# One layer with lagged attention beside a gated feed-forward: q and k of all tokens first, then v, z, o and Wout by halves, with v and z in three f32r passes

## The chip, the cores and the metric

The kernel runs on one core of a Trainium2 chip. The metric is the device time of one execution in microseconds, as the median of the runs. Durations below come from one execution that the hardware profiler recorded.

The engines are called by these names: PE (TensorE) multiplies matrices, DVE (VectorE) and ACT (ScalarE) work on elements, POOL (GpSimd) and SP (SyncE) issue most of the DMA transfers here. Each engine takes its instructions in the order in which they stand in the program.

## What is computed

`x` has 2048 tokens of 512 numbers, everything in f32. The layer is

```python
xn = layernorm(x)
q, k, v = (conv4(silu(xn @ W)) for W in (Wq, Wk, Wv))   # 2048 channels, causal conv over 4 tokens
z, a, b = xn @ Wz, xn @ Wa, xn @ Wb                     # a, b: one number per head
q, k = normalised(rope(q)), normalised(rope(k))         # 16 heads of 128
for s in range(4):                                      # four lags
    attn = sum_over_head(q * lag(k, s)) / sqrt(128)
    o += attn * sigmoid(lag(a, s) * b) * lag(v, s)
s = (o * rms(o) * norm_w * silu(z)) @ Wout
g = silu(relu(xn @ sign(up).T * up_scale) @ sign(down).T * down_scale * output_scale)
out = x + s * g
```

## The kernel before

Tokens go in four blocks of 512, heads in eight pairs (256 channels, two tiles of 128 by 512). Activations lie with channels on the partitions and tokens along the row. `xnT` holds the normalised tokens of all blocks in SBUF.

**Matmuls.** A matmul here has 128 rows of contraction, 128 output rows and 512 columns. The products with Wq, Wk, Wv, Wz and Wout are f32: 256 matmuls each. The profile shows every f32 matmul as two records. The feed-forward is f32r: its weights are signs, and `in_two_terms` splits the other operand into a high and a low term, so that 512 matmuls make up the up-projection and 512 the down-projection, each one record.

**Order.** `InOrder` keeps matmuls, all VectorE work, some ScalarE work (`act`) and some transfers (`pool`, `sp`) in the order in which the program names them. The rest is placed by the scheduler. `step(p, b)` runs pair `p`: q and k of block `b+1` (`queries`, `products`) beside v, z, o and Wout of block `b` (`values`, `weighted`, `gated_output`, `output_projection`). So a first row of eight steps with `b = -1` has q and k of block 0 alone. Beside those stands the feed-forward of block 0, in groups of four of its 16 hidden tiles: `ups` in even steps, `downs` in odd ones, half of it between pq and pk, and half after pk. There the signs are made on ScalarE from the raw weights (`sign`) and also written to `signs_dram`.

**Products and their sums.** `products` turns q for the four lags, multiplies q by the lagged k on VectorE and leaves the sum over the head to a matmul with 0/1 columns (`sum_dots`). In block 0 VectorE adds the two halves of the channels. In later blocks DMAs with accumulation, issued on POOL, do part of it: in an even step `pr1` onto `pr` (L452), then two half sums within `pr` (L469), which wait for the first to land; in an odd step two copies into the pair's tile (L472), then two half sums onto them (L473), which wait for the copies. `sq` (L435) is summed by such a DMA too.

**Between the stages.** The dots, the norms and the gates of a block become coefficients, which go to `co_dram` and come back spread over the partitions as `bc`; `weighted` multiplies v by them.

**Last stage.** After the last step come v, z, o and Wout of block 3, and then the feed-forward of blocks 1 to 3 with the signs loaded from `signs_dram` (`up`, `first_down`, `down`), its ends (`ends`) between.

Of the kernel before, what the change touches and what calls it, by code (L numbers as in the profile page):

```python
# [17 lines left out]
P = 128  # L45
# [3 lines left out]
D = 128  # L49
# [12 lines left out]
ROPE_BASE = 1000000.0  # L62
EPS_LN = 1e-5
# [18 lines left out]
def recurrent_layer(ctx: ExitStack, tc: tile.TileContext, a: dict, out: bass.AP):  # L82
# [10 lines left out]
    xnT = const.tile([P, KC, HALO + S], F32, name="xnT")  # L93
    ss_acc = const.tile([P, NT], F32, name="ss_acc")
# [23 lines left out]
    f_dram = dram.tile([TB, HID], F32, name="f_dram")  # L118
# [3 lines left out]
    att = ctx.enter_context(ExitStack())  # L122
    mm = ctx.enter_context(tc.tile_pool(name="mm", bufs=6, space=PSUM))
# [8 lines left out]
    nc.vector.memset(xnT[:, :, 0:HALO], 0.0)  # L132
# [15 lines left out]
    gates = {}  # L148

    def first_layer_norm():  # L150
# [23 lines left out]
        def transpose(c):  # L174
            tp = mm.tile([P, KC, P], F32, tag="mm", name=f"tp{c}")
            for k in range(KC):
                pe.transpose(tp[:, k, :], x_in[:, c, k * P : (k + 1) * P], ident)
            act.copy(xnT[:, :, HALO + c * P : HALO + (c + 1) * P], tp)
# [20 lines left out]
    def statistics(b, c):  # L199

        if c == 0:
            means[b] = qks.tile([P, TC, 2], F32, tag="mv", name=f"mv{b}", bufs=2)
            nc.sync.dma_start(xnT[:, :, HALO + b * TB : HALO + (b + 1) * TB], a["xT"][b])
# [26 lines left out]
    def centre(b):  # L230
# [9 lines left out]
        for k in range(KC):  # L240
            nc.gpsimd.dma_start(
                xnT[:, k : k + 1, HALO + b * TB : HALO + (b + 1) * TB], less, accum_op=ALU.add
            )

    def divide(b):

        rstd = qks.tile([P, TB], F32, tag="rq", name=f"rstd{b}", bufs=1)
        nc.sync.dma_start(rstd, ln_dram[b][1].partition_broadcast(P))
        at = xnT[:, :, HALO + b * TB : HALO + (b + 1) * TB]
        dve.tensor_tensor(at, at, rstd.unsqueeze(1).to_broadcast([P, KC, TB]), ALU.mult)  # L250

    def gate_products(b):
# [3 lines left out]
        for k in range(KC):  # L256
# [3 lines left out]
                xnT[:, k, HALO + b * TB : HALO + (b + 1) * TB],  # L260
# [70 lines left out]
    def first_product(to, second_half):  # L331

        pps = [mm.tile([P, TB], F32, tag="mm", name=f"pq{j}_0_0") for j in range(2)]
        for lo in range(0, TB, TB // 2):
            for j in range(2):
                for k in range(KC):
# [3 lines left out]
                        xnT[:, k, HALO + lo : HALO + lo + TB // 2],  # L340
# [8 lines left out]
    def project(n, p, b, to):  # L349
# [3 lines left out]
        for j in range(2):  # L353
            pp = mm.tile([P, TB], F32, tag="mm", name=f"p{n}{j}_{p}_{b}")
            for k in range(KC):
# [3 lines left out]
                    xnT[:, k, HALO + b * TB : HALO + (b + 1) * TB],  # L359
# [181 lines left out]
    gated = {}  # L541
    o_due = []

    def squares_of_o():
        while o_due:
            o_due.pop(0)()

    def values(p, b, raw):

        v = sum_with_halo(vs, "v", p, b)  # L550
        convolve(2, p, raw, v[:, :, HALO:])
        return v

    wos = {}

    def load_wo(p, b):
        wo = vs.tile([P, 2, HID], F32, tag="wo", name=f"wo_{p}_{b}", bufs=3)
        loads["by"].dma_start(wo, a["wo"][p])
        wos[p] = wo

    def gates_of_output(p, b):

        z = vs.tile([P, 2, TB], F32, tag="z", name=f"z_{p}_{b}", bufs=1)
        project("z", p, b, z)
        for j in range(2):
            nc.scalar.mul(z[:, j, :], z[:, j, :], norm_w[:, p, j : j + 1])
        return z

    def weighted(p, b, v):

        n = f"_{p}_{b}"
        parts = []
        for lo in range(0, LAGS, 2):

            bc = vs.tile([P, 2, TB], F32, tag="bc", name=f"bc{lo}" + n, bufs=3)
            for h in range(2):
                row = co_dram[b][lo : lo + 2, 2 * p + h, :]
                sp.dma_start(
                    bc[h * D // 2 : (h + 1) * D // 2], row.partition_broadcast(D // 2)
                )  # L580

            v0 = v[:, :, lo : lo + TB]
            v_lags = bass.AP(v0.tensor, v0.offset, [v0.ap[0], [1, 2], *v0.ap[1:]])
            te = vs.tile([P, 2, 2, TB], F32, tag=f"te{lo}", name=f"te{lo}" + n, bufs=1)
            dve.tensor_tensor(te, v_lags, bc.unsqueeze(2).to_broadcast([P, 2, 2, TB]), ALU.mult)
            parts.append(te)
        dve.tensor_tensor(parts[0], parts[0], parts[1], ALU.add)
        o = parts[0][:, 0]
        dve.tensor_tensor(o, o, parts[0][:, 1], ALU.add)


        o2 = xnT[:, p % 2 * 2 : p % 2 * 2 + 2, HALO : HALO + TB] if b else parts[1][:, 0]

        def square():
            (act if b else nc.scalar).activation(o2, o, AF.Square)
            if p == 0:
                pool.dma_start(o2_dram[b], o2)
            else:
                pool.dma_start(o2_dram[b], o2, accum_op=ALU.add)

        if b:
            o_due.append(square)
        else:
            square()
        return o

    def gated_output(p, b, o, z):

        oz = vs.tile([P, 2, TB], F32, tag="oz", name=f"oz_{p}_{b}", bufs=3)
        dve.tensor_tensor(oz, o, z, ALU.mult)  # L610
        gated[p] = oz
        if p % 2 == 1:
            pairs = gated.pop(p - 1), gated.pop(p)
            outputs_due.append(lambda *midway: output_projection(p, b, pairs, *midway))

    def output_projection(p, b, pairs, midway, chunks):

        ws = wos.pop(p - 1), wos.pop(p)
        for c in range(TC):
            if midway and c == chunks:  # L620
                midway()
            po = mm.tile([P, HID], F32, tag="mm", name=f"po{c}_{p}_{b}")
            for i, (of, w) in enumerate(zip(pairs, ws)):
                for j in range(2):
                    pe.matmul(
                        po,
                        of[:, j, c * P : (c + 1) * P],
                        w[:, j, :],
                        start=(i == 0 and j == 0),
                        stop=(i == 1 and j == 1),  # L630
                    )
            part = vs.tile([P, HID], F32, tag="part", name=f"part{c}_{p}_{b}", bufs=4)
            nc.scalar.copy(part, po)  # L633
            t = b * TC + c
            rows = s_dram[t * P : (t + 1) * P, :]
            if p == 1:
                nc.gpsimd.dma_start(rows, part)
            else:
                nc.gpsimd.dma_start(rows, part, accum_op=ALU.add)


    ss = xnT[:, :, HALO + TB : HALO + 2 * TB]

    def load_squares(b, j):

        if j:
            pool.dma_start(ss[:, b], o2_dram[b][:, j], accum_op=ALU.add)
        else:
            loads["by"].dma_start(ss[:, b], o2_dram[b][:, j])

    def output_projections(midway=None, chunks=TC // 2):
        if midway and not outputs_due:
            midway()
        while outputs_due:
            outputs_due.pop(0)(midway, chunks)
            midway = None


    first_due = []

    z_due = []

    def step(p, b, beside_q=None, beside_k=None):
# [4 lines left out]
        squares_of_o()  # L668
        if x_due:
            x_due.pop()()  # L670
        rv = with_halo(vs, "rv", "raw", 1, p, b) if p == b == 0 else None
        if beside_q:
            beside_q()
        if change and b:
            sum_squares(p)
            norms(b)
        due = bool(dots_due) and dots_due[0][-1]
        if change and not b:

            def beside_k():  # L680
                norms(b)
                norms_in_rows(b)

        products(p, b + 1, q, (lambda: norms_in_rows(b)) if change and b else None, beside_k)
        if z_due:
            z_due.pop()()
        if at:
            load(vs, "v", p, b)
            raw = raw_of(vs, "v", p, b, 1, rv)
        if first_due:  # L690
            first_due.pop()()
        if at:
            v = values(p, b, raw)

        def strips():

            if p and p % 2 == 0:
                sum_squares(p)
            if p == NP - 2 and b + 2 < NTB:
                gate_products(b + 2)  # L700
            if p == 1 and not at:
                gate_products(0)
            if due:
                sum_dots()

        z = []
        z_of = lambda: z.append(gates_of_output(p, b))

        early = p == 2 and b == 0
        if early:  # L710
            load(vs, "z", p, b)
            z_of()

        output_projections(strips if p % 2 == 0 or due else None)
        if change:
            coefficients(b)
        if at:
            if not early:
                load(vs, "z", p, b)
            load_wo(p, b)  # L720
            out_of = lambda: gated_output(p, b, weighted(p, b, v), z[0])
            if change:
                z_due.append(z_of)
                first_due.append(out_of)
            else:
                if not early:
                    z_of()
                out_of()
# [41 lines left out]
    def tokens(b):  # L770
        return xnT[:, :, HALO + b * TB : HALO + (b + 1) * TB]

# [403 lines left out]
```

## Time and profile before

| | |
|---|---|
| median of 3 runs | 1399.08 us (1397.86 to 1400.22) |
| span of the profiled execution | 1396.2 us |
| median less that span | 2.9 us |
| PE busy | 1384.6 us (99%) |
| DVE busy | 1179.6 us (84%) |
| ACT busy | 670.2 us (48%) |
| POOL busy | 235.8 us (17%) |
| DMA | 263.40 MB, mean 189 GB/s |

Times on the page and in the views are microseconds from the start of the span unless marked ns. A busy time is a union: records of pipelined matmuls overlap, so their mean duration is longer than the distance between their starts. "Idle before" is the time in which an engine stood before an instruction, with what ended it. "POOL a <- DMA b" in the table of waits reads: POOL, before its instruction on a, waited for the transfer b, with total, number and longest. Where a helper records an operation, its line is that of the helper (L76 before, L53 after).

### The profile page before, as it was taken

The numbers are of one execution on the slowest core, as the hardware profiler recorded it, in microseconds if no ns is written. First come the engines' busy times: TensorE is split into PE (matmuls) and PEld (weight loads), VectorE is DVE, ScalarE is ACT, GpSimd is POOL, SyncE is SP. The second block draws the span as 40 slices with busy tenths as digits, with TensorE's granted clock in tenths as the row PEclk, the third lists the DMA queues.
The fourth block names the chain that finished last, engine by engine and source line by source line (L and its number), as shares of the span: only waits on it lengthen the run. The fifth ranks groups of instructions, "written<-read, shape, count | busy, mean of one in ns | idle before, by whom it ended". The sixth has DMA issues, their size and how long they took to land.

```text
span 1396.2 us, 12500 instructions
## 1 busy us (share of the span) xinstructions
PE 1384.6 (99%) x3962; PEld 689.3 (49%) x3962; DVE 1179.6 (84%) x1183; ACT 670.2 (48%) x1309; POOL 235.8 (17%) x317
## 2 busy tenths in 40 slices
PE   9999999999999999999999999999999999999998
PEld 6555544444444444444444444444444444578886
DVE  7998989999899989998998999989994987337454
ACT  7566646546454564565545544545443443223122
POOL 2222111112213121113131112111111122200000
PEclk9999999999999999999999999999999999999999
DMA  9979577888988789889987798887848989754120
GB/s 319 329 177 206 127 186 178 231 199 205 237 194 190 164 165 243 219 201 197 214 183 163 171 235 203 210 183 179 179 91 204 272 219 243 145 192 139 33 91 31
DMA packets 104985, 263.40 MB, mean 189 GB/s; under 512 B 17812, under 2 KB 18324, under 8 KB 100568
## 3 DMA queue, kind: packets, MB, share of 16 engines
q0 software_dynamic: 36672, 108.02, 39.9%
q1 hardware_dynamic: 68248, 154.58, 37.1%
q8 instruction: 32, 0.52, 0.2%
q14 instruction: 33, 0.27, 0.1%
HBM read 159.77 MB, written 52.45 MB: 152 GB/s over the span
## 4 chain that ended last, share of the span: by engine, by line
PE 88%; DVE 5%; DMA 4%; ACT 1%; issue 1%; SPq 1%; POOL 0%; DVEq 0%; ACTq 0%; POOLq 0%
PE pq L76 15%; PE pk L76 15%; PE po L76 14%; PE pz L76 14%; PE pv L76 13%; PE pf L76 7%; PE ph L76 7%; DVE te L76 1%; PE dots L76 1%; DVE q L76 1%; PE squares L76 1%; DMA y<-s_dram 1%; DVE v L76 1%; DMA bc<-co_dram 1%; DVE k L76 0%
## 5 line engine op out<-in xcount | busy, mean ns | idle before, releaser
L76 PE MATMUL pq<-xnT,wq 128*128 128x512 f32 (+1 forms) x528 | 226.1, 580 | 0.8 <-ACT rstd L76 0.8
L76 PE MATMUL po<-wo,oz 128*128 128x512 f32 x512 | 225.6, 595 | 0.0
L76 PE MATMUL pz<-xnT,wz 128*128 128x512 f32 x512 | 225.2, 592 | 0.4 <-ACT rv L363 0.4
L76 PE MATMUL pk<-xnT,wk 128*128 128x512 f32 x512 | 225.2, 592 | 0.0
L76 PE MATMUL pv<-xnT,wv 128*128 128x512 f32 x512 | 225.2, 592 | 0.0
L76 DVE TENSOR_TENSOR te<-v,bc 128x2048 f32<-128x2048 f32 x64 | 143.9, 2288 | 33.8 <-ACT v L76 15.8
L76 DVE SCALAR_TENSOR_TENSOR k<-rk,conv_w,k 128x512 f32<-128x512 f32 x192 | 141.7, 751 | 30.5 <-ACT k L375 26.0
L76 PEld LDWEIGHTS pq<-xnT,wq 128*128 128x128 f32 x528 | 99.0, 189 | 123.6 <-issue 115.1
L76 PEld LDWEIGHTS po<-wo,oz 128*128 128x128 f32 x512 | 96.2, 190 | 126.5 <-issue 115.4
L76 PEld LDWEIGHTS pz<-xnT,wz 128*128 128x128 f32 x512 | 96.6, 189 | 123.9 <-issue 118.0
L76 PEld LDWEIGHTS pv<-xnT,wv 128*128 128x128 f32 x512 | 96.6, 189 | 123.8 <-issue 119.9
L76 PEld LDWEIGHTS pk<-xnT,wk 128*128 128x128 f32 x512 | 96.6, 189 | 120.6 <-issue 118.0
L76 DVE SCALAR_TENSOR_TENSOR q<-rq,conv_w,q 128x512 f32<-128x512 f32 x192 | 141.5, 749 | 17.1 <-ACT q L375 12.5
L76 DVE SCALAR_TENSOR_TENSOR v<-rv,conv_w,v 128x512 f32<-128x512 f32 x192 | 141.3, 750 | 6.4 <-ACT v L375 1.9
L76 DVE SCALAR_TENSOR_TENSOR q<-q,turns 128x1024 f32<-128x1024 f32 (+1 forms) x128 | 127.3, 1016 | 4.9 <-ACT q L76 2.6
L76 DVE TENSOR_TENSOR pr<-q,k 128x2048 f32<-128x2048 f32 x52 | 117.3, 2287 | 0.9
L76 DVE CAST hid_hi<-hid 128x512 fp32r<-128x512 f32 x52 | 22.4, 431 | 88.2 <-ACT hid L785 88.2
L785 ACT ACTIVATE hid<-ph,up_scale 128x512 f32<-128x512 f32 x64 | 43.5, 684 | 105.6 <-PE ph L76 104.3
L363 ACT ACTIVATE rq<-pq 128x512 f32<-128x512 f32 x62 | 36.8, 596 | 93.3 <-PE pq L76 93.2
L633 ACT COPY part<-po 128x512 f32<-128x512 f32 x64 | 36.9, 579 | 82.7 <-PE po L76 82.7
L76 PE MATMUL ph<-xs_hi,up 128*128 128x512 f32 x192 | 75.5, 393 | 0.0
L76 PE MATMUL ph<-xs_lo,up 128*128 128x512 f32 x192 | 74.7, 389 | 0.0
(154 smaller groups left out, 1744.6 us busy)
## 6 DMA issues: line engine op xcount, KB each, us to landing
bc<-co_dram SPq DMA_DIRECT2D x128, 256.0 KB
pr<-pr POOLq DMA_DIRECT2D x72, 256.0 KB, 6.9
wq<-in_wq_dram SPq DMA_DIRECT2D x32, 512.0 KB
wk<-in_wk_dram SPq DMA_DIRECT2D x32, 512.0 KB
sq<-sq POOLq DMA_DIRECT2D x32, 512.0 KB, 6.5
wv<-in_wv_dram SPq DMA_DIRECT2D x32, 512.0 KB
wz<-in_wz_dram SPq DMA_DIRECT2D x32, 512.0 KB
wo<-in_wo_dram SPq DMA_DIRECT2D x32, 512.0 KB
```

What stands on the lines that cost most here:

```text
L76: return self.tc.keep_in_program_order(getattr(self.engine, op)(*args, **kwargs))
L363: nc.scalar.activation(to[:, j, :], pp, AF.Silu)
L633: nc.scalar.copy(part, po)
L785: nc.scalar.activation(hid, ph, AF.Relu, scale=scale)
```

## The change

The work is laid out in two stages.

**Stage one: all q and k.** `step` has only q and k left. It runs for all four blocks, 32 steps in all, and each block has its own feed-forward beside it, as block 0 had before. `f_dram` grows to all tokens. In block 0 signs are made as before. For the later blocks each group of signs (1 MB) is read back from `signs_dram` by a `pool` transfer, called at the end of the step before the one that uses it, into one of two buffers:

```python
def fetch(b, g, which):
    if b:
        of = signs[which] = signs_of(b, g, which)     # tag "sign", bufs=2
        pool.dma_start(of, signs_dram[which][:, G * g : G * g + G])
        return
    ...
for b in range(NTB):
    for p in range(NP):
        ...
            step(p, b - 1, lambda: ups(...), lambda: ups(...))      # odd p: downs
        ...
        if n + 1 < len(groups) and groups[n + 1][0]:
            fetch(*groups[n + 1])
```

`xnT` is gone: each block of tokens has a tile of its own. Each block is also cut into three f32r forms, `h` (the value times 1 - 2^-13, rounded), `m` (value minus h) and `d` (h - 4096 m). `h` and `m` serve the feed-forward as its two terms, and all three are written to `forms_dram` (3 MB a block).

**Stage two: v, z, o, Wout**, for halves of 1024 tokens, eight pairs each (16 rounds). It starts when the pools of stage one are released. The forms of two blocks are loaded as `xf`; the weights of v and z are split on the way (`split_raw`: two ScalarE and two VectorE operations of 128 by 1024). A tile of v or z is then

```python
for k in range(KC):                       # form d with form d, 4 matmuls
    pe.matmul(pp, wd[:, k, ...], xf[b, 2][:, k], start=(k == 0), stop=(k == KC - 1))
nc.scalar.mul(pp, pp, -1.0 / (UNIT + 1.0))
for k in range(KC):                       # h with h and m with m, 8 matmuls on top
    for t, w in ((0, wh), (1, wm)):
        pe.matmul(pp, w[:, k, ...], xf[b, t][:, k], start=False, ...)
```

and 1 + 1/4096 goes into the scale of the Silu that reads it. That is 12 f32r matmuls for 4 f32 ones. `gated_outputs(i - 1)`, one half of an `output_projection`, and `raw_values(i)` follow each other in round `i`; Wout begins in round 3.

**The end.** The final gate (`end`) of the first half stands in rounds 12 to 15, two tiles in each, with one buffer each for `x`, `y` and `g`. The last half's is done at the end, where the last eight chunks of Wout are read from PSUM directly. `roots` sums the squares of o by a matmul ahead of those chunks.

The core of the diff:

```diff
-    xnT = const.tile([P, KC, HALO + S], F32, name="xnT")
+    xnp = ctx.enter_context(tc.tile_pool(name="xnp", bufs=4))
+    wfp = ctx.enter_context(tc.tile_pool(name="wfp", bufs=4, side="right"))
-    f_dram = dram.tile([TB, HID], F32, name="f_dram")
+    f_dram = dram.tile([S, HID], F32, name="f_dram")
+    forms_dram = [dram.tile([P, 3, KC, TB], F32R, name=f"forms_dram{b}") for b in range(NTB)]
...
     def step(p, b, beside_q=None, beside_k=None):
...
-        if at:
-            load(vs, "v", p, b)
-            raw = raw_of(vs, "v", p, b, 1, rv)
-        if first_due:
-            first_due.pop()()
-        if at:
-            v = values(p, b, raw)
...
+    def split_raw(n, i):
+        pool, w = w_raws.pop((n, i))
...
+        nc.scalar.activation(h, w, AF.Copy, scale=LOW)
+        dve.tensor_tensor(m, w, h, ALU.subtract)
+        dve.scalar_tensor_tensor(d, m, -UNIT, h, ALU.mult, ALU.add)
+        nc.scalar.mul(m, m, UNIT)
...
+    def project_forms(n, i, evict):
...
+    for i in range(n_all + 1):
+        s, p = divmod(i, NP)
+        if i:
+            gated_outputs(i - 1)
...
+        if i > 2:
+            m, h = (i - 2, 0) if i % 2 else (i - 3, 1)
+            output_projection(m, h)
...
+        if i < n_all:
+            raw = raw_values(i)
+            split_raw("z", i)
...
+            v = values(i, raw)
+            for h in range(2):
+                weighted(i, h, v)
```

## The prediction

> **What bounds the kernel now.** I read the page's first part and its groups first, then the chain of waits in order of time, then what POOL waited for and POOL's and VectorE's timelines.
>
> ```profile
> span 1396.2 us, 12500 instructions
> ...
> PE 1384.6 (99%) x3962; PEld 689.3 (49%) x3962; DVE 1179.6 (84%) x1183; ACT 670.2 (48%) x1309; POOL 235.8 (17%) x317
> ...
> L76 PE MATMUL pv<-xnT,wv 128*128 128x512 f32 x512 | 225.2, 592 | 0.0
> ```
>
> TensorE is the bound: it idles 11.6 us in all. The program has 256 v products and the group counts 512, so one f32 matmul is two records, 225.2/256 = 0.88 us. The chain gives the prices back to back, in the opening stretch where q and k run beside the feed-forward (columns: start, length, what):
>
> ```profile
> 145.86 7.07 PE pq L76 x16
> 152.93 3.66 PE ph L76 x16
> 156.59 6.87 PE pk L76 x16
> 163.46 3.67 PE ph L76 x16
> 169.84 7.07 PE pq L76 x16
> ```
>
> Eight f32 matmuls take 6.87 us (0.859 each), 16 f32r ones 3.67 us (0.229 each). A step of this stretch lasts 23.1 us (pq starts at 53.73 and, six steps later, at 192.13). This is the new kernel's first stage already at work, and here VectorE is as full as TensorE (39.3 us busy of the 40 from 120 to 160). What the stretch lacks is the reading of stored signs, since block 0 makes them on the spot, and the summing of pr by DMA, which only later blocks do. That is seen further on, on POOL (idle in brackets):
>
> ```profile
> 226.16 0.85 POOL L452 DMA_DIRECT2D pr<-pr  x1 [11.41 <-DVE pr L76]
> 235.74 1.56 POOL L469 DMA_DIRECT2D pr<-pr  x2 [8.73 <-DMA pr<-pr]
> ...
> 252.35 1.02 POOL L472 DMA_DIRECT2D pr<-pr  x2 [9.28 <-DVE pr L76]
> 257.09 0.79 POOL L473 DMA_DIRECT2D pr<-pr  x1 [3.72 <-DMA pr<-pr]
> 258.09 0.79 POOL L473 DMA_DIRECT2D pr<-pr  x1 [0.21 <-issue]
> ```
>
> and in the table of waits:
>
> ```profile
> POOL pr L469 <- DMA pr<-pr: 115.7, 12, 14.6
> ...
> POOL pr L473 <- DMA pr<-pr: 56.1, 21, 7.5
> ```
>
> POOL stands still until its own earlier transfer has landed, 9.6 us each time at L469. Today nothing that TensorE needs soon is behind it.
>
> **What is saved.** v and z are 512 f32 matmuls; three f32r passes cost 3 x 0.229 = 0.688 us for 0.859, so 0.171 x 512 = 88 us. q, k, Wout and the feed-forward keep their counts. VectorE gains the weight splits (32 x 2.5 us) and loses little.
>
> **What the move adds: the signs' load becomes a link in every step.** In blocks 1 to 3 of the new first stage, `fetch` reads 1 MB of signs for step n+1 on POOL at the end of step n. In the order in which the changed program's instructions stand on POOL, nearly all these loads come after the pr sums of step n; on TensorE the matmuls that need them stand between pq and pk of step n+1. So the loop closes: signs land, half the feed-forward, pk, the convolution, turn and products on VectorE, the pr sums on POOL, the next load. pq is the only large work that TensorE can do meanwhile. Queued behind POOL's wait are the load, then sq and f_dram; TensorE waits for the load.
>
> *From signs landed to products done.* 3.67 (half the feed-forward) + 6.87 (pk), then the tail, which the last q/k step shows with VectorE nearly free:
>
> ```profile
> 1018.64 2.33 DVE L76 SCALAR_TENSOR_TENSOR k<-rk,conv_w,k 128x512 f32<-128x512 f32 x3 [1.10 <-ACT k L375]
> 1020.88 4.05 DVE L76 SCALAR_TENSOR_TENSOR q<-q,turns 128x512 f32<-128x512 f32 x4
> 1024.96 2.29 DVE L76 TENSOR_TENSOR pr<-q,k 128x2048 f32<-128x2048 f32 x1
> 1027.17 2.29 DVE L76 TENSOR_TENSOR q<-q,k 128x2048 f32<-128x2048 f32 x1
> 1029.49 2.29 DVE L76 TENSOR_TENSOR pr<-pr,q 128x2048 f32<-128x2048 f32 x1
> ```
>
> There pk ended at 1017.22 and the products at 1031.78: 14.6 us. Odd step: 3.67 + 6.87 + 14.6 = 25.1. An even step has two products for three (-2.29) and two hid_lo (+1.29): 24.1. The first step of blocks 2 and 3 has the norms before turn (216.36 to 221.45): 5.1 more.
>
> *From products done to signs landed.* After an even step: the products ended at 225.87 and POOL's two half sums were issued by 237.30, so 11.4; after an odd one 252.04 to 258.88, so 6.8. Then the load. The nearest row is the one 1 MB read of stored signs, queued behind another POOL sum (transfers with KB and us to landing):
>
> ```profile
> first_down<-down_signs POOLq DMA_DIRECT2D x1, 1024.0 KB, 7.9
> ```
>
> Together 19.3 and 14.7. Bounds: L469's quickest case was 8.56 us from issue, and half-size sign reads had 8.3 as median in traffic, so 6 is the least that I allow for the load; that gives 16.3 and 12.0. Its slowest ordinary case, 11.8, with 9.9 for the load (the three 1 MB reads of down) gives 23.6; odd, with L473 finishing 10.8 after its products and 9.9, 20.7. The Trainium skill, "DMA: Bandwidth & Descriptors", section "Anatomy of one DMA", puts such a POOL transfer at 2.0 us plus its bytes over 436 GB/s. By it the 1 MB load is an estimated 4.4 us, and 23 steps would be 80 us shorter in all. The row decides, since it was queued behind a sum just as here.
>
> Two loads in blocks 1 and 2 stand a little earlier: the fifth behind the layer norm's four DMAs, which wait for a reciprocal after the products, the seventh ahead of L452's half sums but behind the ab chain. I count them at the same price.
>
> **Sum.** Block 0 goes as now: the products of step (0, block 1) end at 225.9. From there 12 even and 11 odd waits and 12 odd and 11 even steps: 12 x 19.3 + 11 x 14.7 + 12 x 25.1 + 11 x 24.1 + 2 x 5.1 = 970. The products of the last step end at 1196. In the hidden case these 23 steps would take 23.1 each, 531: the loop costs 439 us.
>
> *The join.* After the products: half sums and their landing 6.8 + 4.7, dots 1.1, the norms' chain meanwhile, two coefficient steps 1.4, co_dram 6.2 (the chain has that row), then xf1 into the released space, 2 MB behind each other, 7.9 + 3.3: 32 us, in which TensorE has some 10 of work. v starts at 1228.
>
> *v, z, o, Wout.* TensorE per weight pair: 11.0 + 11.0 + 16 x 0.859 = 35.8. VectorE: convolution 7.7, weighting 16.2, oz 2.5, splits 5.0 = 31.4. In the first three rounds Wout is not yet there and VectorE leads: v(0) ends 5.5 after the start, z(2) can begin after two VectorE rounds, at +67. Thirteen rounds of 35.8 make +532. Four of them carry two `end` each, with one buffer for x, y, g: VectorE waits for a store and a load (about 6 us, estimated from 2.2 to 2.9 us for the small ss transfers in the chain) and does 4.2 more, 41.6 against 35.8: +20 (bounds 0 and 45). Last: weighting of pair 15, its square and two transfers of o2 (5.8 and 4.9 in the chain) before roots' matmul, 37 us; eight chunks 27.5; 4 to the end. 1228 + 532 + 20 + 69 = 1849.
>
> *Cold restarts.* TensorE now stands some 20 us in each of 23 steps. The trace hardly shows it after a pause; its nearest row is the start, where the first six records took 3.9 us for 2.2 of work at the later pace: 1.7 more. Nothing at one end, 1.7 x 23 = 38 at the other. I take the 38, as each pause is long. 1887, and with the 2.9 us by which the median stands above this profile's span, 1890. I give 1885.
>
> **Rivals.**
> - *The signs are hidden (not slower).* If each load is served during the step before, the 23 steps run at 22.3 to 23.1 us (the shortest and the mean step of block 0), 513 to 531 for 970, and the cold price goes: 1885 - 38 - (457 to 439) = 1390 to 1408. The join, the VectorE-led rounds and the tail eat most of the 88 us. I name 1390, since later blocks sum dots half as often. It decides from the point where a load is issued about 13 us before the products end: pq ends some 5 us before them in block 0 (177 and 182.6), and the load takes 7.9. For it: the DMA engines have room. Against it: the order on POOL, and 9.6 us of standing still at L469. Chance 0.05.
> - *A lighter chain.* In the pauses little else is moved, so sums and loads go at the quick bounds: 12 x 3.0 + 11 x 2.7 = 66 less, and no cold price: 1780. Chance 0.13.
> - *A heavier chain.* The forms' 3 MB of writes per block, the layer norm's sums and the xf loads fall into the same queue: 12 x 4.3 + 11 x 6.0 = 118 more: 2005. Against: they stand behind the signs' load, not ahead of it. Chance 0.10.
>
> **How the numbers follow.** The forecast has 0.72. The range leaves out the hidden case and half of each end: 1775 to 2000. About 0.2% can be told from no change. Faster has the hidden case's larger part, 0.03; same 0.01; slower 0.96.
>
> **What would show it.** Right: blocks 1 to 3 with steps of 38 to 46 us, TensorE half idle there with ph and pf waiting for a DMA from the sign stores, POOL waiting at the pr half sums just before; v and z matmuls near 0.23 us; rounds of 36 us later. Wrong: steps of 23 us in block 2; or f32r passes that cost more than 0.23 us; or a second stage far from 620 us, which would point to ScalarE's in-order evictions, where I see 28 us of work in 36.

## The result and the profile after

| | before | after |
|---|---|---|
| median of 4 runs each | 1398.47 us (1396.38 to 1400.22) | 2067.97 us (2063.05 to 2069.85) |
| ratio | 1 | 1.478 (95% interval 1.475 to 1.480) |
| span of the profiled execution | 1396.2 us | 2068.1 us |
| mean granted TensorE clock | 0.999 | 0.832 |

The change costs 669 us; the forecast was 486, and the measured time lies 68 us above the end of the range. The page of the changed kernel (busy time in us and share; the third line gives the granted clock in tenths, in 40 slices of 52 us; then two groups, with busy time, mean ns and the idle time before them):

```profile
span 2068.1 us, 13579 instructions
...
PE 1388.7 (67%) x4474; PEld 833.7 (40%) x4474; DVE 1231.9 (60%) x1119; ACT 861.6 (42%) x1503; POOL 269.0 (13%) x369
...
PEclk9999767797777779777778776789999869998877
...
L53 PE MATMUL ph<-xs_h,up 128*128 128x512 f32 x256 | 123.1, 481 | 262.3 <-DMA up<-up_signs 262.3
L53 PE MATMUL pf<-down,hid_hi 128*128 128x512 f32 x256 | 123.2, 481 | 226.3 <-DMA down<-down_signs 226.3
```

TensorE was 99% busy and is 67% busy. No engine has taken its place: 488.6 us of its idle time stand before two groups, ph and pf, and a load of signs ends them. The clock falls where these waits lie (slices 5 to 27). The table of waits has the same, and POOL's waits ahead of the loads (total, number, longest):

```profile
PE ph L53 <- DMA up<-up_signs: 262.3, 12, 27.1
...
PE pf L53 <- DMA down<-down_signs: 226.3, 10, 28.5
...
POOL pr L452 <- DMA pr<-pr: 85.0, 12, 9.5
...
PE so L53 <- DMA ss<-o_dram: 60.1, 2, 36.9
...
POOL pr L456 <- DMA pr<-pr: 50.7, 20, 6.6
...
DVE g L53 <- DMA g<-f_dram: 46.3, 4, 14.7
```

POOL's timeline of one odd step (L455 and L456 are L472 and L473 of before) and the first matmul on TensorE that needs the signs:

```profile
298.84 1.02 POOL L455 DMA_DIRECT2D pr<-pr  x2 [9.25 <-DVE pr L53]
303.88 0.78 POOL L456 DMA_DIRECT2D pr<-pr  x1 [4.01 <-DMA pr<-pr]
305.04 0.77 POOL L456 DMA_DIRECT2D pr<-pr  x1 [0.39 <-DMA pr<-pr]
305.55 0.86 POOL L53 DMA_DIRECT2D up<-up_signs  x1
```

```profile
317.00 0.76 PE L53 MATMUL ph<-xs_h,up 128*128 128x512 f32 x1 [25.14 <-DMA up<-up_signs]
```

The products end at 298.55, the two half sums hold POOL until 305.5, the load lands at 317. This is the loop of the prediction. From landing to landing its steps last 41 to 57 us, and 25 us in the two that do not wait; the mean of the 23 from 211.11 to 1255.61 is 45.4 us, for 43.8 in the sum with the cold restart.

The second stage, v of round 0 at 1320.7 to the end, takes 747 us for 621. TensorE's timeline has four kinds of stop there that the forecast did not price, or priced too low: the entry to the second half of the tokens, roots(0), the rounds of the last gates (one of three shown), and roots(1) (idle time and its end in brackets):

```profile
1611.80 2.04 PE L53 MATMUL pv<-xf,wv_d 128*128 128x512 f32 x4 [12.77 <-DMA xf<-forms_dram]
...
1707.86 1.92 PE L53 MATMUL so<-ss,ones 128*32 128x512 f32 x2 [36.93 <-DMA ss<-o_dram]
...
1917.54 2.93 PE L53 MATMUL pz<-xf,wz_d 128*128 128x512 f32 x6 [13.25 <-DVE wz_d L53]
...
2015.87 1.91 PE L53 MATMUL so<-ss,ones 128*32 128x512 f32 x2 [23.17 <-DMA ss<-o_dram]
```

Where nothing stops it a round is what was forecast: v begins at 1737.46, 1773.27, 1808.79 and 1844.64, 35.7 us apart.

### The profile page after: what moved, and what is told of

The parts are those of the page before. It is cut to its first block, busy times and chain, and to the rows that moved or that the text cites. A ratio compares the mean times of both kernels' runs of the same rounds, so it can differ in the third digit from the quotient of the medians.

```text
span 2068.1 us, 13579 instructions
## 1 busy us (share of the span) xinstructions
PE 1388.7 (67%) x4474; PEld 833.7 (40%) x4474; DVE 1231.9 (60%) x1119; ACT 861.6 (42%) x1503; POOL 269.0 (13%) x369
## 4 chain that ended last, share of the span: by engine, by line
PE 28%; DVE 23%; DMA 22%; issue 19%; ACT 4%; POOL 3%; SPq 1%; DVEq 0%; POOLq 0%; ACTq 0%
PE pk L53 7%; DVE q L53 6%; PE pz L53 5%; DMA pr<-pr 5%; DVE pr L53 5%; DMA down<-down_signs 5%; PE po L53 4%; DVE k L53 4%; PE pv L53 4%; DMA up<-up_signs 4%; PE pf L53 3%; PE ph L53 3%; DMA xf<-forms_dram 2%; DVE te L53 2%; PE pq L53 2%
## 5 line engine op out<-in xcount | busy, mean ns | idle before, releaser
L53 PE MATMUL ph<-xs_h,up 128*128 128x512 f32 x256 | 123.1, 481 | 262.3 <-DMA up<-up_signs 262.3
L53 PE MATMUL pf<-down,hid_hi 128*128 128x512 f32 x256 | 123.2, 481 | 226.3 <-DMA down<-down_signs 226.3
L53 PE MATMUL pq<-xn,wq 128*128 128x512 f32 (+1 forms) x528 | 229.0, 587 | 2.9 <-DMA wq<-in_wq_dram 2.6
L53 PE MATMUL pk<-xn,wk 128*128 128x512 f32 x512 | 225.3, 593 | 0.0
L53 PE MATMUL po<-wo,o 128*128 128x512 f32 x512 | 224.4, 597 | 0.0
L53 DVE SCALAR_TENSOR_TENSOR v<-rv,conv_w,v 128x1024 f32<-128x1024 f32 x96 | 122.0, 1284 | 87.3 <-ACT v L839 85.1
L53 PEld LDWEIGHTS pq<-xn,wq 128*128 128x128 f32 x528 | 99.1, 191 | 126.2 <-issue 112.2
L53 PE MATMUL pf<-down,hid_lo 128*128 128x512 f32 x256 | 112.6, 440 | 2.1 <-DVE hid_lo L53 2.1
L53 PE MATMUL ph<-xs_m,up 128*128 128x512 f32 x256 | 112.7, 440 | 1.5 <-DVE xs_m L53 1.5
L53 PE MATMUL pv<-xf,wv_h 128*128 128x512 f32 x256 | 103.3, 404 | 11.4 <-DVE wz_d L53 8.8
```

The source lines that it names most:

```text
L53: return self.tc.keep_in_program_order(getattr(self.engine, op)(*args, **kwargs))
```

## The experiments

Each is one run with a profile. Four runs of the changed kernel lie within 7 us, and two edits below that leave the first stage alone still have their first v matmul 5.9 us earlier and 5.5 us later than the changed kernel. So a difference under some 12 us says nothing here.

**The sign load a step early.** Theory: the load stands behind POOL's sums. Rival: loads are slow whenever they are asked for.

```diff
                 n = b * NP + p
+                if n + 1 < len(groups) and groups[n + 1][0]:
+                    fetch(*groups[n + 1])
                 if n == 0:
                     step(p, -1, first_signs, lambda: ups(0, 0, G))
...
-                if n + 1 < len(groups) and groups[n + 1][0]:
-                    fetch(*groups[n + 1])
```

> The sign load of step n+1 is issued at the start of step n, ahead of that step's sums of the products, instead of after them; nothing else is touched. Theory (GpSimd holds the load behind sums that wait for a DMA, and TensorE waits for the load): the waits of ph and pf for the signs (262 + 226 us in the changed kernel) all but vanish, and the steps of blocks 1 to 3, 44.8 us on average from 211 to 1285 us, fall to 25 to 30 us, which VectorE's 24 us of work a step and TensorE's set. 24 x (44.8 - 27) = 427 us less: 1640 us, 1590 to 1690. Rival (the load is late whenever it is asked for, because the DMA engines or the queue are the limit): at most 100 us less, over 1950 us, and the waits stay.

Measured: 1651.5 us, 416 less. No buffer was added: the second one is free from the start of the step. Its waits:

```profile
PE ph L53 <- DMA up<-up_signs: 25.6, 7, 6.3
...
PE pf L53 <- DMA down<-down_signs: 14.0, 3, 5.1
```

and the windows of the changed kernel and of this one over the steps (bounds and length, busy us of PE, PEld, DVE, ACT and POOL with instructions, granted clock, DMA share, GB/s):

```profile
211.00:1200.00 989.00, 533.69 (x1608) 297.01 (x1608) 474.17 (x488) 322.99 (x630) 142.12 (x193) 0.77 0.55 121
```

```profile
211.00:878.00 667.00, 562.39 (x1746) 305.46 (x1745) 509.14 (x524) 342.24 (x669) 153.58 (x207) 0.91 0.83 189
```

The 488.6 us of waits are 39.6, and the DMA engines carry 189 GB/s for 121. The rival is out. The first v matmul comes at 878 us for 1297, 419 us earlier, so the whole gain is in the first stage.

**The sums on VectorE, the load where it was.** This separates the two things that the early load changes at once: what stands before the load on POOL, and where the program calls it.

```diff
-        if not b or p % 2 == 0:
+        if True:
             pr1 = ...
             product(pr1, 1, 0, LAGS)
-            if b:
-                nc.gpsimd.dma_start(pr, pr1, accum_op=ALU.add)
-            elif p < NP - 1:
+            if p < NP - 1:
                 dve.tensor_tensor(pr, pr, pr1, ALU.add)
...
-        if not b:
+        if True:
             dots_due.append([p, prs, of_head[:, p], p == NP - 1, True])
             return
```

> Blocks 1 to 3 add the two product tiles on VectorE and leave the halves to TensorE's head sums, as block 0 does; the load keeps its place at the end of the step, but GpSimd's queue no longer holds a sum that waits for a DMA. Theory: the place in the program costs little by itself, the sums in front of it do; steps of 27 to 30 us (VectorE 2.3 us more in every even step, the head sums 16 more f32 matmuls of 0.86 us a block), 24 x (44.8 - 29) = 380 us less: 1690 us, 1630 to 1760. Rival (the load is late because the program asks for it only at the end of the step before): the load still lands after the first half of the next step's q products, the waits stay above 250 us in all, and the time stays above 1850 us.

Measured: 1715.2 us, 353 less; 108 us of waits for signs are left. The call can stay at the end of the step: once nothing ahead of it on POOL waits for a transfer, POOL reaches it while the step is still running (the load of one odd step is issued at 272.00, and VectorE is done with that step's products and their sum at 282.4). What cost the time was the sums in front of it.

**A quarter of the load.**

```diff
-                pool.dma_start(of, signs_dram[which][:, G * g : G * g + G])
+                pool.dma_start(of[:, 0:1], signs_dram[which][:, G * g : G * g + 1])
```

> Each sign load of blocks 1 to 3 brings a quarter of its bytes (0.25 MB for 1 MB), and the feed-forward uses that quarter for all four chunks of the group, so that its values are left out for the rest. Theory: the load itself stands in the loop of every step, 10.5 us from issue to landing; at 0.25 MB it takes about 5 us (between the accumulating writes of 0.25 MB and half), so 22 steps fall by 5.5 us each: 120 us less, 1950 us, 1900 to 1990. Rival 1 (a load costs its start, not its bytes): under 30 us less. Rival 2 (the page's 2.0 us plus bytes by 436 GB/s): 1.8 us a step, 40 us less, 2030 us.

Measured: 2007.3 us, 61 less, half of the theory and neither rival. The two DMA views (KB each, median us from issue to landing), changed kernel first:

```profile
up<-up_signs POOLq DMA_DIRECT2D x12, 1024.0 KB, 10.2
down<-down_signs POOLq DMA_DIRECT2D x12, 1024.0 KB, 10.7
```

```profile
up<-up_signs POOLq DMA_DIRECT2D x12, 256.0 KB, 7.2
down<-down_signs POOLq DMA_DIRECT2D x12, 256.0 KB, 7.2
```

So 3.0 to 3.5 us go with 0.75 MB. A straight line through these two sizes leaves about 6 us of a load that do not depend on its bytes; a third size was not tried. The load is in the loop with its full length, but a smaller one could not have saved the kernel.

**Idle matmuls in the wait.** Is the slow clock a cause or only a sign?

```diff
         if beside_q:
+            if at and p != 5:
+                keep_warm()          # 88 matmuls of 128 x 128, into an unread bank
             beside_q()
```

> Before the first half of the feed-forward of each step of blocks 1 to 3 but p = 5 (which does not wait in blocks 1 and 2), 88 matmuls of 128 x 128 f32 into a bank that nobody reads, some 19 us of TensorE, in place of most of its wait for the signs. Theory: the clock granted in blocks 1 to 3 rises from 0.77 to over 0.95, the first half of the feed-forward, 5.6 to 6.6 us after the wait, falls to 3.7 to 4.2, and the k products too run at full clock: 3 us a step, 60 to 80 us less, 1990 to 2010 us. Rival 1 (the slow restarts are covered by VectorE's and ScalarE's chain): within 15 us of 2068. Rival 2 (the idle work overruns the short waits at p = 1 and delays the loop): some 10 us given back.

Measured: 2083.5 us, 16 more. The granted clock from 211 to 950 rose from 0.77 to 0.95, and nothing was gained: 15 of the 19 halves that waited for signs still began cold, after idle times of 1.9 to 20.8 us that the idle work had left open. The edit had not removed what it was to price, so it was run again with the idle work cut to each step's wait (13 to 121 matmuls):

> As the run with 88 idle matmuls in each step, but with as many in each step as its wait in the changed kernel had room for, less 1.2 us (0.2251 us each: 13 to 121, none in the two steps that do not wait), so that TensorE stands still for 0 to 2 us before each half of the feed-forward and not for 3 to 9. Theory (a restart is cold after 2.9 us of idle time as after 28, and not after 1.8): the first 16 matmuls of a half take 3.7 to 3.8 us again, for 5.6 on average, the granted clock of blocks 1 to 3 is over 0.97, and 22 x 1.9 = 42 us go: 2026 us, 2015 to 2045. Rival (the restart costs nothing, because VectorE's and ScalarE's chain covers it, or the idle work delays as much as it saves): within 12 us of 2068, or above.

Measured: 2042.5 us, 25 less; the granted clock over the steps is 0.99. The same half of the feed-forward, changed kernel first:

```profile
317.00 0.76 PE L53 MATMUL ph<-xs_h,up 128*128 128x512 f32 x1 [25.14 <-DMA up<-up_signs]
317.56 0.63 PE L53 MATMUL ph<-xs_m,up 128*128 128x512 f32 x1
317.99 0.63 PE L53 MATMUL ph<-xs_h,up 128*128 128x512 f32 x1
```

```profile
310.34 0.47 PE L53 MATMUL ph<-xs_h,up 128*128 128x512 f32 x1 [1.50 <-DMA up<-up_signs]
310.65 0.40 PE L53 MATMUL ph<-xs_m,up 128*128 128x512 f32 x1
310.88 0.39 PE L53 MATMUL ph<-xs_h,up 128*128 128x512 f32 x1
```

Starts are 0.43 us apart after 25.1 us of idle time and 0.23 after 1.5. Of 22 halves 18 began warm, so 18 x 1.9 = 34 us were to be had and 25 to 28 came (the last landing is 27.6 us earlier). The rest was not traced.

**The carried columns of k.** In the changed kernel the products end 17.2 us after pk in the odd steps of blocks 1 and 2, and 14.6, the forecast's figure, in those of block 3. Block 3 carries nothing over to a next block.

```diff
         q0 = q[:, LAGS - 1]
+        if "k" in to_keep:
+            to_keep.pop("k")()
         raw = raw_of(qks, "k", p, b)
```

> The copy that carries the last three columns of k over to the next block is issued before the k products instead of after them, so that the next k tile is free sooner and ScalarE can multiply the first half of k between its two evictions. Theory: this copy is why the products of blocks 1 and 2 end 16.0 (even) and 17.2 us (odd) after the k products, for 13.3 and 14.6 in block 3, which carries nothing over; the 15 steps of blocks 1 and 2 that wait fall by 2.6 us each: 40 us less, 2028 us, 2020 to 2040. Rival (block 3 is shorter for another reason, the layer norms or the gates that it lacks): within 12 us of 2068, and the 17.2 us stay.

Measured: 2028.9 us, 39 less; the tails of blocks 1 and 2 are 14.8 (odd) and 13.5 us (even). ScalarE's timeline of the same step, changed kernel first:

```profile
277.91 0.60 ACT L346 ACTIVATE rk<-pk 128x512 f32<-128x512 f32 x1 [2.85 <-PE pk L53]
281.35 0.60 ACT L346 ACTIVATE rk<-pk 128x512 f32<-128x512 f32 x1 [2.84 <-PE pk L53]
...
282.08 0.19 ACT L53 COPY kept_k<-k 128x6 f32<-128x6 f32 x1
...
282.41 1.33 ACT L358 ACTIVATE k<-rk,conv_w 128x512 f32<-128x512 f32 x2
```

```profile
265.30 0.20 ACT L53 COPY kept_k<-k 128x6 f32<-128x6 f32 x1
268.25 0.60 ACT L346 ACTIVATE rk<-pk 128x512 f32<-128x512 f32 x1 [2.75 <-PE pk L53]
268.88 0.72 ACT L358 ACTIVATE k<-rk,conv_w 128x512 f32<-128x512 f32 x1
271.69 0.60 ACT L346 ACTIVATE rk<-pk 128x512 f32<-128x512 f32 x1 [2.08 <-PE pk L53]
```

`k` has one buffer, so its next tile cannot be written before the 0.2 us copy has read the last one. Behind the second eviction, that copy keeps the first half's multiplication, and with it half of VectorE's convolution, 2.4 to 2.5 us late in a loop that has nothing to hide it.

**roots(0) out of the way.**

```diff
-        ss = vs.tile([P, 2, TB], F32, tag="o2", name=f"ss{s}")
+        halves[s] = [vs.tile([P, TB], F32, tag="xy"[h], name=f"ss{s}_{h}") for h in range(2)]
...
+        if i == NP + 1:
+            load_halves(0)          # ahead of weighted(i)
...
-        if i == NP + 1:
+        if i == NP + 2:
             roots(0)
```

> The halves of the squares of o for roots(0) are loaded into buffers of x and y at the start of round 9, ahead of that round's two stores of o2 on GpSimd, and roots(0) with its matmuls stands a round later. Theory: the 36.9 us for which TensorE stands at so in round 9 are a queue position, on GpSimd behind the o2 stores of round 9 and in the one o2 buffer behind its square; they go and nothing takes their place, and the start of v(9) to the start of v(10) falls from 78.3 to 36 to 41 us: 37 to 42 us less, 2028 us, 2020 to 2036. Rival (VectorE is as late as so in that round, since it also converts, weights and waits): the round stays over 55 us and the time over 2045 us.

Measured: 2044.1 us, 24 less, between the theory and its rival. Round 9, from v to v, fell from 78.3 to 35.9 us as the theory said: the 36.9 us were a place in a queue. But the second stage as a whole began 5.5 us later than in the changed kernel, ahead of anything that the edit touches, so's own matmuls moved into round 10 (3.6 us), and the last so now waits longer:

```profile
1991.01 1.91 PE L53 MATMUL so<-ss,ones 128*32 128x512 f32 x2 [29.66 <-DMA ss<-o_dram]
```

29.7 us for 23.2: its halves now need the buffers of the last gates. That reason was read from the program and not tried by itself.

**Four f32r passes for three.**

```diff
-            for k in range(KC):
-                pe.matmul(pp, wd[...], xf[2 * s + h, 2][:, k], ...)
+            for _ in range(2):
+                for k in range(KC):
+                    pe.matmul(pp, wd[...], xf[2 * s + h, 2][:, k], ...)
```

> The first of the three f32r passes of every v and z product runs twice over, its first result overwritten, so that a product has four f32r passes: 512 matmuls of 128 x 512 more, at 0.229 us 117 us of TensorE. Theory: TensorE sets the rounds 3 to 12, 7.3 us more in each; the first three rounds, in which z waits 6.7 us for wz_d, and the last three, in which it waits 9.7 to 13.2 us, hide most of theirs: 75 to 95 us more, 2150 us. Rival (VectorE or ScalarE sets the rounds, and the passes saved are hidden): under 40 us more.

Measured: 2129.5 us, 61 more, under the theory and over its rival. The rounds that TensorE sets went from 35.8 to 43.1 us, 7.3 as expected (v begins at 1408.87, 1452.08, 1495.23 and 1538.01). The rest went into waits, by more than I had counted: rounds 0 to 2 lost all of theirs, the entry to the second half stood 7.0 us at its first wait for 12.8, and the rounds with gates took up most of theirs. So a further pass (117 us of TensorE) costs about half of its length in this kernel. Counted from the first v matmul to the end it costs 66 us, since this run's second stage began 5.9 us earlier.

**All edits together.** The early signs, the early roots, the early copy of k, and the second half's forms loaded ahead of round 7's last o2 store.

> Four edits together: the sign loads a step early, the loads of roots(0) ahead, the copy of k ahead, and the six loads of the second half's forms ahead of the last o2 store of round 7 (which then comes after them on GpSimd). Theory: the gains lie in different stretches and add up, but the copy of k is worth little where TensorE no longer waits for the signs: 1651.5 - 40 (roots) - 8 (forms) - 0 to 20: 1595 us, 1575 to 1610. Rival (the early loads make the edits compete for GpSimd's queue): over 1630 us. By either the time stays far above that of the kernel before.

Measured: 1581.6 us, beside 1401.5 for the kernel before on the same chip: 486 us less than the changed kernel and 1.13 times the kernel before. The forms loaded ahead bring little: TensorE's first wait for them falls from 12.8 to 1.6 us, but the six loads land behind each other and three later ones still stop it for 2.9 to 3.3 us, so that rounds 7 and 8 last 92.1 us for 97.8. No version here beats the kernel before. Its largest waits on TensorE:

```profile
PE pz L53 <- DVE wz_d L53: 45.9, 5, 12.9
PE so L53 <- DMA ss<-o_dram: 30.1, 1, 30.1
PE dots L53 <- DMA pr<-pr: 28.5, 5, 12.1
PE ph L53 <- DMA up<-up_signs: 23.8, 7, 5.7
```

None of them would bring the missing 180 us. What is left is spread over the opening rounds of the second stage, its gates with one buffer each, and its tail.

## Why the prediction was wrong

The direction was right, and so was the mechanism of the first stage; the second stage failed in a step of its own. The load of signs behind POOL's sums is what made the kernel slow: moving the load alone took 416 us back, and the sums on VectorE showed that what stands in front of it did it. Against the forecast of 1885 us 183 were missing. In the sum itself (1887 us of span, measured 2068.1) they are 181: 55 before v starts (1266 with the cold restarts, measured 1320.7) and 126 after. By its steps:

- **The price of v and z.** Right: v and z matmuls start 0.227 us apart (1641.07 to 1643.79 for twelve), and free rounds last 35.7 us. How much of the 88 us is left on the path was not tried by itself: a fourth pass costs about half of its time, which does not tell what the pass taken away saved.
- **The opening.** "Block 0 goes as now": the products of step (0, block 1) were to end at 225.9 and ended at 248.3, 22 us later. 7.9 of them were lost before that step: block 0 did not go as before, and the step's pq starts at 199.94 for 192.06. The other 14.5 are in it: I took its length from a step without the feed-forward of block 1 beside it. The first half of that feed-forward stands before pk, waits 4.0 us for the first load and takes 8.4 us.
- **From signs landed to products done.** This term was mis-sized by its tail, 14.6 us. The row that I took it from is the last q/k step, which carries no columns over; blocks 1 and 2 do, and have 2.6 us more in 15 steps (39 us; the early copy gave 39 back). From landing to the end of pk was 12.8 us, in odd steps as in even ones after the first, for 12.2 with the cold restart, some 12 us in all.
- **From products done to signs landed.** From the products to the issue of the load was shorter in even steps and equal in odd ones (means 9.3 and 6.9, for 11.4 and 6.8), but the load was longer: 10.2 to 10.7 us for 7.9, and above the 9.9 of the upper bound. Odd waits were 17.5 for 14.7 (about 31 us in all), ordinary even ones 20.0 for 19.3. That the even price nearly held is in part luck: in the kernel before, the twelve even sums took 10.4 to 20.8 us after the products, and 11.4 is one of the quickest; the 11.8 from L452 to L469, which I called the slowest ordinary case, is near the median of 8.6 to 17.8. The Trainium skill, "DMA: Bandwidth & Descriptors", section "Anatomy of one DMA", gives, as an estimate from its fit of 2.0 us plus the bytes over 436 GB/s, 4.4 us for this load and 2.6 for a quarter of it. Measured are 10.2 to 10.7 and 7.2: by the line through both, the fixed part is about 6 us for 2.0, and a MB more costs 4.0 to 4.7 us for 2.4. The measurement decides.
- **The fifth and seventh loads at the same price.** Wrong, and to my favour. The fifth (`down` for p = 5 of blocks 1 and 2) stands behind the layer norm's transfers but ahead of its step's sums; it was issued at 409.50, before the products of that step ended at 441.75, and nobody waited. It saved some 22 us twice, the seventh 6 us twice.
- **The join.** 37.6 us for 32.
- **Cold restarts.** Right: 38 us forecast; the 21 halves after the first loads took 5.65 us for 3.75, 1.9 us each. The reason "as each pause is long" was wrong: 3 us of idle time cost as much as 28.
- **Thirteen rounds without a stop.** This is the step that failed most. I took all rounds at the price of a free one (13 x 35.8, +20 for `end`) and never asked what the program does between the halves. At the entry to the second half TensorE waits for its six forms, which POOL loads after round 7's o2 store: round 8 lasts 47.4 us and the one before it 50.4, 26 us over two free rounds. The place behind that store makes about 6 of the 26 (all edits together); what the other 20 hang on was not tried by itself. roots(0), which I had priced only in its second copy, stops TensorE for 36.9 us in round 9, with its matmuls 42. Its own experiment took that round back to 35.9, and the total fell by 24 us. Both stops were terms that the sum put at nothing.
- **`end`.** Forecast +20 (0 to 45): the three rounds that it lengthens last 48.2, 51.3 and 48 us, +40 in all, inside the bounds and at twice the value. g waits up to 14.7 us for its load, where I had estimated 6.
- **The tail.** From z of the last round: 102 us for 69. so comes 50 us after that z for 37; its eight chunks and the gates after them 52 for 32. That makes 33 us more. These last three steps are 121 of the 126 us after v starts.

The rivals of the forecast fell too. "A heavier chain" (2005) came nearest, but the waits that it raises stayed under its 23.6 and 20.7 us (20.0 and 17.5), and no run tried its reasons. "The signs are hidden" was priced at 1390; the early load is nearly that case (39.6 us of waits left), and it is 1651.5. The loop was only one of the costs: with it gone, v begins in full at 901.7 us where that case had 771 to 789 (the opening, and steps of some 27 us for 23.1), and the second stage has its 127 us more as before. The range could not hold the result because both ends were built from the loop alone; the second stage had a bound for one term in it. One sign of being wrong, a second stage far from 620 us, did come (747), but not for the reason given with it, ScalarE's evictions: free rounds last 35.7 us, as forecast.

## What to carry to other kernels

A DMA call at the end of a step is not issued at the end of the step: it is issued when everything in front of it on its engine has stopped waiting. Look up what those waits are, and call the load before them if its buffer is free. When a plan is split into halves, price every switch between them, and every small reduction placed in an in-order matmul stream, as well as the steady round. A row taken from the last block may lack what all other blocks do.

## What the runs showed of the hardware

- **Restarts.** In the fitted run the first 16 matmuls of a half took 3.72 to 3.83 us after 18 idle times of 0.80 to 2.52 us, and 5.33 to 6.40 us after three of 2.71 to 3.23 us. A fourth slow one, after 2.31 us, had a second wait of 1.09 us behind its first matmul. In the changed kernel, after 15 to 28 us, they took 5.07 to 6.47. One half of the run with 88 idle matmuls was cold after 1.9 us. So in these runs the price of a pause sets in somewhere between 1.9 and 2.7 us, and does not grow from there. The slow matmuls need not come first: after the pauses of 1.92, 2.71 and 3.23 us two to five matmuls still ran at full pace before the slow ones. In the fitted run the mean granted clock over the steps is 0.99, in the changed kernel 0.77.
- The Trainium skill, "TensorE: Matmul & The Clock Gate", Part 1, puts the window for going cold and for warming up at about 3.4 us each, free-running. The slow part here was 6 to 13 matmuls of 0.43 us, 2.6 to 5.6 us; pauses of 1.9 and 2.7 us already brought it, shorter than one such window. The measurement decides.
- **Loads.** A 1 MB load from DRAM on POOL's queue took 10.2 to 10.7 us from issue to landing, 0.25 MB 7.2 us, at 0.52 to 0.55 of the DMA engines' time: by a straight line through these two sizes, about 6 us do not depend on the size.
